# Attention b's stream: each query group divided by its sums in four small parts, a batch's output given out in three passes

## The chip, the core and the metric

The kernel runs on one core of a Trainium2 chip. The core has a matrix engine (TensorE, called PE in the profile, with its weight loads as PEld), three engines for elementwise work (VectorE or DVE, ScalarE or ACT, GpSimd or POOL) and DMA queues, of which this kernel uses the one of SyncE (SP). Matmul results go to PSUM[...]. The metric is the device time of one execution in microseconds, lower is better.

## What is computed

Two layers on x of 2 batches x 512 tokens x 512 values, all fp32, each layer an attention and then a small mixture of experts, each with a layer norm ahead and added to x:

```python
x = x + attn_a(layernorm(x))    # 32 heads of 128, 8 key heads, 4-bit weights, rope, causal
x = x + ffn(layernorm(x))       # 8 experts of rank 64, the best two of a softmax gate
x = x + attn_b(layernorm(x))    # 32 heads of 16, 8 key heads, rope, causal
x = x + ffn(layernorm(x))
```

The change lies in attention b and in what is laid beside it:

```python
att = einsum('bhgqd,bhkd->bhgqk', q, k) / sqrt(16)      # g: the 4 query heads of a key head
probs = softmax(where(causal, att, -inf))
out = einsum('bhgqk,bhkd->bhgqd', probs, v)
return concat_heads(out) @ Wo
```

## The kernel before

Attention a comes first (to about 720 us), then the first experts ("f1"), then attention b, then the second experts ("f2").

**Units of attention b.** A unit is (batch b, query group g of 4, half kh of the key heads): 2 x 4 x 2 = 16 units, 4 heads in each, one on each strip of 32 partitions. Two streams walk the units. `maxima` (lines 653 to 676) multiplies queries by keys (`sc_b`, L668) and takes the row maxima on DVE (L672) into a spare column of `qpads`. `probabilities` (681 to 712), some 8 steps later, makes the transposed scores less the maximum (`st_b`, L694), takes exp on ACT (L700) and clears the part over the diagonal on POOL (L704). Both take their PSUM banks from the one pool `ps_x` of five banks, so a score that has not been read yet keeps the next from being made. `weighted_b` (714 to 745) multiplies the probabilities by the values (`num_b`, L721). The values carry a column of ones, so the row sums come out as row 16 of each strip.

**Sums and division.** When a unit's four products are done, ACT copies the result to SBUF: for kh = 0 into `oN[b, g]`, for kh = 1 into a temporary tile. Four DMAs on SP's queue bring the four rows of sums into a tile `dens` (L738), and for kh = 1 four more bring the values beside those of kh = 0 (L745). Before the change one tile `dens[b, 0]` collects the sums of the groups 0 to 2 of a batch and `dens[b, 1]` those of group 3, each after a memset on POOL (L735). `divided(b, late)` (747 to 757) takes the reciprocal of such a whole 128x512 tile on DVE (L750), then for each of its groups spreads the rows over the strips (`stream_shuffle`, L755) and multiplies (L756).

**Output.** `output_b(b)` (759 to 769) first runs `divided(b, 1)`, then for each of 4 token tiles accumulates the four groups' products with `wo2` in one PSUM bank `po` (L764) and adds it to x on DVE (L768).

**The order.** The loop of lines 798 to 835 goes through 104 steps (96 of 16 units x 6, and LEAD = 8 more), with `half` = 48. Inside it the order on PE is the written order (`manual_schedule`); the order on the other engines is made by the planner that builds the program. A step does two pieces of each stream, two thirds of a `weighted_b` (the queue `due`), and side work: a generator `side`, whose parts name their cost (0.9 for some 0.86 us of matmuls), is advanced until the `pace` of the step is used up:

```python
            left += pace
            while left > 0:
                got = next(side, None)
                if got is None:
                    left = 0.0
                else:
                    left -= got
```

Side work is first the rest of batch 1's first experts and its projections (pace 1.35, to step 46), then nothing until step 59, then batch 0's output and second experts (pace 1.25). `divided(0, 0)` is run whole at step 49, `divided(1, 0)` at step 97. After the loop come batch 1's output, what is left of the side work, and batch 1's second experts (840 to 844). Outside the loop the planner orders PE too. A part of the projections puts rotations on DVE (L579, L581); an experts' layer begins with a norm, whose square root makes ACT load another table.

Of the kernel before, what the change touches and what calls it, by code (L numbers as in the profile page):

```python
# [11 lines left out]
F32 = mybir.dt.float32  # L12
# [3 lines left out]
ALU = mybir.AluOpType  # L16
# [3 lines left out]
P = 128  # L20
B, S, DM = 2, 512, 512
# [10 lines left out]
B_NH, B_NKV, B_HD = 32, 8, 16  # L32
B_G = B_NH // B_NKV
# [8 lines left out]
def kernel(  # L42
# [21 lines left out]
    nc = tc.nc  # L64
# [63 lines left out]
    with ExitStack() as actx:  # L128
# [192 lines left out]
        def chain(*stages):  # L321
            for stage in stages:
                yield from stage
# [11 lines left out]
        for n in range(len(units) + 4):  # L335
            turn = []

            def at(lag):
                if 0 <= n - lag < len(units):
                    g, b, h = units[n - lag]  # L340
                    return (g, b, h, f"{g}_{b}_{h}")

            if at(3):
                g, b, h, nm = at(3)
# [4 lines left out]
            if at(0):  # L349
                g, b, h, nm = at(0)  # L350
# [8 lines left out]
            if at(4):  # L359
                g, b, h, nm = at(4)  # L360
                turn.append(output(wo[g], h, g * A_G + h, b, *ats.pop((g, b, h)), nm))
            if at(2):
                g, b, h, nm = at(2)
# [37 lines left out]
    wo2 = w2.tile([P, B_G, DM], F32, tag="wo2", name="wo2")  # L401
# [32 lines left out]
    temps = ctx.enter_context(tc.tile_pool(name="temps", bufs=4))  # L434
    wep = ctx.enter_context(tc.tile_pool(name="we", bufs=2))
    gate = ctx.enter_context(tc.tile_pool(name="gate", bufs=1))
    bp = ctx.enter_context(tc.tile_pool(name="b", bufs=1))
# [9 lines left out]
    def bank(shape, name):  # L447
        pool, tag = (ps_x, "x") if shared["on"] else (ps_f, "f")
        return pool.tile(shape, F32, tag=tag, name=name)
# [4 lines left out]
    MM = 0.9  # L454
# [136 lines left out]
    def projections(b):  # L591

        xT = yield from norm_parts(b, "b")


        kT = kTs[b] = bp.tile([P, 2, S], F32, tag=f"kT{b}", name=f"kT_b_{b}")
        v = vpads[b]
        for t in range(NT):
            nm = f"b_{b}_{t}"
            kpad = kpads[t % 2]  # L600
            pq = bank([P, DM], f"pq_{nm}")
            for c in range(NC):
                nc.tensor.matmul(  # L603
                    pq, xT[:, c, ts(t, P)], wq2[:, c, :], start=(c == 0), stop=(c == NC - 1)
                )
                if c == NC - 1:
                    rope_heads(qpads[b, t], pq, B_NH, t, 2, f"q{nm}")
                yield MM
            pkv = bank([P, DM], f"pkv_{nm}")
            for c in range(NC):  # L610
                nc.tensor.matmul(
                    pkv[:, :256], xT[:, c, ts(t, P)], wkv2[:, c, :], start=(c == 0), stop=(c == NC - 1)
                )
                if c == 1:
                    yield MM
            rope_heads(kpad, pkv[:, 0:128], B_NKV, t, 0, f"k{nm}")
            for kh in range(2):
                nc.scalar.copy(
                    v[:, t, kh, :, :B_HD],
                    pkv[:, 128 + kh * 64 : 192 + kh * 64].rearrange("p (s d) -> p s d", d=B_HD),  # L620
                )
            yield 3 * MM
            tp = bank([P, 2, P], f"tpk_{nm}")
            kf = kpad.rearrange("p h d -> p (h d)")
            for c in range(2):
                nc.tensor.transpose(tp[:, c, :], kf[:, ts(c, P)], ident)
            nc.scalar.copy(kT[:, :, ts(t, P)], tp)
            yield 0.2
# [18 lines left out]
    STEPS, LEAD, HELD = 6, 8, 1  # L647
    qTm, qTp, nums, oNs = {}, {}, {}, {}


    dens = {}
# [62 lines left out]
    def weighted_b(b, g, j, kh, pT):  # L714


        first, last = j == 0, j == NT - 1
        if first:
            nums[b, g, kh] = ps_n.tile([P, S], F32, tag="num", name=f"num_b_{b}_{g}_{kh}")
        for s in range(4):  # L720
            nc.tensor.matmul(  # L721
                nums[b, g, kh][ts(s, STRIP), j * P :], vpads[b][:, j, kh, s, :], pT[s],
                start=first, stop=last,
            )
        if not last:
            return
        if kh == 0:
            got = oNs[b, g] = bp.tile([P, S], F32, tag=f"oN{b}{g}", name=f"oN_b_{b}_{g}")
        else:
            got = temps.tile([P, S], F32, tag="t", name=f"o1_b_{b}_{g}")  # L730
        nc.scalar.copy(got, nums.pop((b, g, kh)))
        row, late = kh * B_G + g, int(g == B_G - 1)
        if (b, late) not in dens:
            dens[b, late] = bp.tile([P, S], F32, tag=f"dens{late}", name=f"dens_b_{b}_{late}")
            nc.gpsimd.memset(dens[b, late], 1.0)  # L735
        for s in range(4):
            at = s * STRIP
            nc.sync.dma_start(  # L738
                dens[b, late][at + row : at + row + 1, :], got[at + B_HD : at + B_HD + 1, :]
            )  # L740
        if kh == 1:

            for s in range(4):
                at = s * STRIP
                nc.sync.dma_start(oNs[b, g][at + B_HD : at + STRIP, :], got[at : at + B_HD, :])  # L745

    def divided(b, late):

        rden = temps.tile([P, S], F32, tag="t", name=f"rden_b_{b}_{late}")
        nc.vector.reciprocal(rden, dens[b, late])  # L750
        yield 5.0
        for g in (B_G - 1,) if late else range(B_G - 1):
            rb = temps.tile([P, S], F32, tag="t", name=f"rb_b_{b}_{g}")
            rows = [kh * B_G + g for kh in range(2) for _ in range(B_HD)]
            nc.vector.stream_shuffle(rb, rden, rows)  # L755
            nc.vector.tensor_tensor(oNs[b, g], oNs[b, g], rb, ALU.mult)  # L756
            yield MM

    def output_b(b):
        yield from divided(b, 1)  # L760
        for i in range(NT):
            po = bank([P, DM], f"po_{b}_{i}")
            for g in range(B_G):
                nc.tensor.matmul(  # L764
                    po, oNs[b, g][:, ts(i, P)], wo2[:, g, :], start=(g == 0), stop=(g == B_G - 1)
                )
                if g == B_G - 1:
                    nc.vector.tensor_tensor(x[b, i], x[b, i], po, ALU.add)  # L768
                yield MM

    def run(*stages):
        stages = list(stages)
        while stages:
            stages = [st for st in stages if next(st, stages) is not stages]
# [5 lines left out]
    def parts(stage, n):  # L780
        for _ in range(n):
            next(stage, None)
# [10 lines left out]
    total = len(units) * STEPS  # L793
    half = total // 2
    shared["on"] = False
    side = chain(later, projections(1))
    pace, left, col = 1.35, 0.0, 0.0
    for step in range(total + LEAD):
        with tc.manual_schedule(engines={mybir.EngineType.PE}):
            if step == half - 2:  # L800
                run(side)
            for b in range(B):

                if step == half * (b + 1) + 1:
                    run(divided(b, 0))
            if step == half + LEAD + 3:
                side = chain(output_b(0), experts(0, "f2", True))
                pace, left = 1.25, 0.0
            for lead in (0, 2):
                k, at = divmod(step + lead, STEPS)  # L810
                if at == 0 and k < len(units) and (lead or step == 0):
                    qTm[units[k]] = transposed(*units[k], "m")
            k, at = divmod(step - STEPS, STEPS)
            if at == 1 and 0 <= k < len(units):
                qTp[units[k]] = transposed(*units[k], "p")

            alone = step < LEAD or step >= total
            for _ in range(4 * (step % 2 == 0) if alone else 2):
                if LEAD <= step:
                    next(ps)  # L820
                if step < total:
                    next(ms)

            col += 2 / 3
            while col >= 1:
                col -= 1
                if len(due) > HELD:
                    due.pop(0)()
# [7 lines that stand above are left out]
    shared["on"] = True  # L836
    while due:
        due.pop(0)()

    last = output_b(1)  # L840
    parts(last, 2)
    parts(side, 5)
    run(last)
    run(side, experts(1, "f2", True))


# [88 lines left out]
```

## Time and profile before

| | us |
|---|---|
| median of 3 runs | 1170.47 (1168.96 to 1172.08) |
| the profiled execution | 1172.71 |
| its span | 1170.7 |
| PE busy | 1107.2 |
| DVE busy | 883.0 |
| ACT busy | 591.7 |
| POOL busy | 525.5 |
| mean granted clock of PE | 0.975 of full speed |

A profile is one execution. "Busy" is the time in which an engine had an instruction running. PE's matmuls overlap and their ends are modelled, so a busy PE may still run below its best. The granted clock is the share of full speed that the chip gave PE; at 0.50 each matmul takes twice as long. A line of the timeline gives the start in us from the span's start, the duration, the engine, the source line and operation, what it writes and reads, the shape, and in brackets how long the engine had stood before it and what ended that. One fp32 matmul of the source is two records. Of attention b's stream, 812 us to 1110 us are the loop; the two streams overlap from 830 to 1085.

### The profile page before, as it was taken

The page shows a single profiled execution, that of the slowest core. Times are in us where ns is not written, and L with a number is a line of the kernel's source. Part 1 is how long each engine was busy: PE and PEld are TensorE (multiplying, and loading weights), DVE is VectorE, ACT ScalarE, POOL GpSimd, SP SyncE. Part 2 cuts the span into 40 slices and gives each one's busy share as a digit, 9 for nine tenths or more (in the row PEclk, how much of TensorE's full clock was granted, in tenths as well). Part 3 has the DMA queues.
Part 4 walks back from the last instruction along what each step waited for, and adds up shares of the span by engine and source line. Part 5 has one row for each costly group of instructions (what it writes and reads, how often), then busy time and mean ns, then how long its engine had stood idle before and what let it go on. Part 6 is the DMA issues. An engine that isn't in the chain of part 4 may idle for free.

```text
span 1170.7 us, 16843 instructions
## 1 busy us (share of the span) xinstructions
PE 1107.2 (95%) x5428; PEld 694.0 (59%) x5428; DVE 883.0 (75%) x2175; ACT 591.7 (51%) x1373; POOL 525.5 (45%) x758
## 2 busy tenths in 40 slices
PE   5799999999999999999999996989999999999998
PEld 3467777777777776777777774444444444444343
DVE  6889899998998999999998887244755676565442
ACT  3566566576656656656566663212254444364410
POOL 1556655665565666566565665111123322222200
PEclk9999999999999999999999998899989978989999
DMA  7301011022001100101100002400000000000000
GB/s 274 108 1 37 1 37 37 1 72 72 3 35 37 37 1 37 38 1 37 37 1 1 1 1 92 76 0 1 2 1 6 6 6 6 7 6 2 15 32 36
DMA packets 13448, 35.07 MB, mean 30 GB/s; under 512 B 4081, under 2 KB 5041, under 8 KB 10801
## 3 DMA queue, kind: packets, MB, share of 16 engines
q1 hardware_dynamic: 13360, 34.01, 8.8%
q8 instruction: 43, 0.70, 0.2%
q14 instruction: 45, 0.36, 0.1%
HBM read 30.72 MB, written 2.10 MB: 28 GB/s over the span
## 4 chain that ended last, share of the span: by engine, by line
PE 86%; DVE 7%; ACT 2%; POOL 2%; issue 2%; DMA 1%; SPq 0%; DVEq 0%; ACTq 0%; POOLq 0%
PE av L280 11%; PE sc L247 11%; PE st_b L694 7%; PE tp L275 6%; PE ps_o L289 5%; PE ps_o L290 5%; PE ps_q L209 5%; PE py_f L563 5%; PE ps_q L210 5%; PE ph_f L504 4%; PE num_b L721 4%; PE po L764 3%; PE pq_b L603 3%; PE sc_b L668 2%; PE ps_k L210 1%
## 5 line engine op out<-in xcount | busy, mean ns | idle before, releaser
L672 DVE CUSTOM_DVE_ANT_0 sc_b<-sc_b,tri 128x128 f32<-128x128 f32 (+3 forms) x256 | 122.6, 510 | 92.2 <-PE sc_b L668 76.6
L255 ACT ACTIVATE p<-sc,nmx 128x128 f32<-128x128 f32 (+3 forms) x256 | 135.5, 529 | 93.9 <-DVE nmx L250 91.8
L247 PE MATMUL sc<-kT,qT 128*128 128x128 f32 (+3 forms) x512 | 179.6, 433 | 1.5 <-POOL qT L228 1.2
L216 DVE SCALAR_TENSOR_TENSOR r_q<-ps_q,s_q,r_q 128x512 f32<-128x512 f32 x192 | 143.7, 749 | 35.8 <-PE ps_q L210 22.4
L227 POOL TENSOR_TENSOR r_q<-r_q,tab 128x512 f32<-128x512 f32 x64 | 82.3, 1286 | 191.1 <-DVE rs_q L226 191.1
L276 ACT COPY pT<-tp 128x128 f32<-128x128 f32 (+3 forms) x256 | 109.3, 427 | 102.2 <-PE tp L275 101.5
L264 POOL TENSOR_SCALAR p<-p,rden 128x128 f32<-128x128 f32 (+3 forms) x256 | 139.2, 556 | 46.2 <-DVE rden L262 22.8
L704 POOL TENSOR_SCALAR_AFFINE_SELECT pT_b<-pT_b 128x128 f32<-128x128 f32 (+1 forms) x192 | 62.7, 331 | 195.2 <-ACT pT_b L700 192.5
L280 PE MATMUL av<-pT,v 128*128 128x512 f32 (+3 forms) x512 | 148.7, 433 | 0.2 <-ACT pT L276 0.2
L280 PEld LDWEIGHTS av<-pT,v 128*128 128x128 f32 x512 | 96.8, 190 | 80.6 <-issue 52.7
L700 ACT ACTIVATE pT_b<-st_b 128x384 f32<-128x384 f32 (+1 forms) x192 | 92.2, 528 | 96.3 <-PE sc_b L668 68.1
L299 DVE SCALAR_TENSOR_TENSOR acc<-ps_o,s_o,acc 128x512 f32<-128x512 f32 x186 | 137.7, 740 | 2.9 <-PE ps_o L290 2.7
L209 PE MATMUL ps_q<-xh,w_q 128*128 128x512 f32 x256 | 122.8, 480 | 7.4 <-DVE r_q L216 7.4
L250 DVE CUSTOM_DVE_ANT_0 sc<-sc,tri 128x128 f32<-128x128 f32 (+3 forms) x256 | 125.7, 491 | 3.5 <-PE sc L247 2.5
L694 PE MATMUL st_b<-qT_b_p,kT_b 32*128 32x256 f32 (+3 forms) x512 | 119.1, 503 | 6.0 <-DVE qpad L672 3.6
L668 PE MATMUL sc_b<-kT_b,qT_b_m 32*128 32x384 f32 (+3 forms) x512 | 118.2, 499 | 1.4 <-ACT qT_b_m L639 0.7
L275 PE MATMUL tp<-ident,p 128*128 128x128 f32 x640 | 112.7, 272 | 2.3 <-POOL p L264 2.3
L247 PEld LDWEIGHTS sc<-kT,qT 128*128 128x128 f32 x512 | 95.3, 189 | 24.3 <-POOL qT L228 1.6
L289 PE MATMUL ps_o<-ah,w_o 128*128 128x512 f32 x256 | 108.3, 424 | 1.1 <-ACT ah L168 0.9
L290 PE MATMUL ps_o<-al,w_o 128*128 128x512 f32 x256 | 103.4, 407 | 3.5 <-DVE al L169 3.5
L210 PE MATMUL ps_q<-xl,w_q 128*128 128x512 f32 x256 | 101.5, 396 | 0.0
L275 PEld LDWEIGHTS tp<-ident,p 128*128 128x128 f32 x640 | 82.8, 140 | 28.9 <-issue 4.8
(175 smaller groups left out, 2010.6 us busy)
## 6 DMA issues: line engine op xcount, KB each, us to landing
codes_q<-in_q_codes_dram SPq DMA_DIRECT2D x8, 1024.0 KB, 4.8
codes_o<-in_o_codes_dram SPq DMA_DIRECT2D x8, 1024.0 KB, 4.8
x_a<-in_x_dram SPq DMA_DIRECT2D x8, 256.0 KB, 6.6
codes_k<-in_k_codes_dram SPq DMA_DIRECT2D x2, 1024.0 KB, 6.3
codes_v<-in_v_codes_dram SPq DMA_DIRECT2D x2, 1024.0 KB, 6.0
x_r<-in_x_dram SPq DMA_DIRECT2D x8, 256.0 KB, 3.5
out_dram<-x_r SPq DMA_DIRECT2D x8, 256.0 KB, 2.1
la<-in_lora_a_dram SPq DMA_DIRECT2D x1, 1024.0 KB, 5.6
```

The lines of the kernel that those rows point to most:

```text
L209: nc.tensor.matmul(ps, w[:, c, ts(h, A_HD)], xh[b][:, c, :], start=True, stop=False)
L210: nc.tensor.matmul(ps, w[:, c, ts(h, A_HD)], xl[b][:, c, :], start=False, stop=True)
L216: nc.vector.scalar_tensor_tensor(r, ps, s, r, ALU.mult, ALU.add)
L247: nc.tensor.matmul(sc[:, :n], qT[:, ts(i, P)], kT[:, :n], start=True, stop=True)
L264: nc.gpsimd.tensor_scalar(prs[j], prs[j], rden[:, j % 2 : j % 2 + 1], 1.0, ALU.mult, ALU.mult)
L275: nc.tensor.transpose(tp[:, j, :], prs[i][:, ts(j, P)], ident)
L280: nc.tensor.matmul(av[:, j * P :], v[:, j, :], pT[:, j, j * P :], start=(j == 0), stop=(j == NT - 1))
L289: nc.tensor.matmul(ps, w[:, h, ts(n, P)], ah, start=True, stop=False)
L290: nc.tensor.matmul(ps, w[:, h, ts(n, P)], al, start=False, stop=True)
L299: nc.vector.scalar_tensor_tensor(to, ps, s, to, ALU.mult, ALU.add)
L668: nc.tensor.matmul(part, qT[strip, ts(i, P)], kT[strip, kh, :n], start=True, stop=True)
L694: nc.tensor.matmul(st[:, at : at + n], kT[strip, kh, ts(j, P)], qT[strip, j * P :], start=True, stop=True,)
```

## The change

The tile `dens` becomes one for each query group and batch (two tags in turn). As soon as a group's second half is done, a generator `divided(b, g)` for it is put into a list `quotients`; each step of the loop advances every generator in the list by one part: two empty parts, the reciprocal of the left 256 columns, that of the right 256, the shuffle, the product. Nothing is divided whole inside the loop any more.

`output_b(b, gs)` makes the output of the groups `gs` only and adds it to x. Batch 0's output comes in three passes: groups 0 and 1 from step 46 (pace 0.6), group 2 chained behind at step 56, group 3 at step 66 with the second experts (pace 1.05). Batch 1's groups 0 and 1 are set ahead of the side work at step 96 (pace 1.6), groups 2 and 3 follow after the loop, behind the last quotient and six parts of side work.

```diff
-        row, late = kh * B_G + g, int(g == B_G - 1)
-        if (b, late) not in dens:
-            dens[b, late] = bp.tile([P, S], F32, tag=f"dens{late}", name=f"dens_b_{b}_{late}")
-            nc.gpsimd.memset(dens[b, late], 1.0)
+        if kh == 0:
+            dens[b, g] = bp.tile([P, S], F32, tag=f"dens{g % 2}", name=f"dens_b_{b}_{g}")
+            nc.gpsimd.memset(dens[b, g], 1.0)
         for s in range(4):
             at = s * STRIP
             nc.sync.dma_start(
-                dens[b, late][at + row : at + row + 1, :], got[at + B_HD : at + B_HD + 1, :]
+                dens[b, g][at + kh : at + kh + 1, :], got[at + B_HD : at + B_HD + 1, :]
             )
...
-    def divided(b, late):
-
-        rden = temps.tile([P, S], F32, tag="t", name=f"rden_b_{b}_{late}")
-        nc.vector.reciprocal(rden, dens[b, late])
-        yield 5.0
-        for g in (B_G - 1,) if late else range(B_G - 1):
-            rb = temps.tile([P, S], F32, tag="t", name=f"rb_b_{b}_{g}")
-            rows = [kh * B_G + g for kh in range(2) for _ in range(B_HD)]
-            nc.vector.stream_shuffle(rb, rden, rows)
-            nc.vector.tensor_tensor(oNs[b, g], oNs[b, g], rb, ALU.mult)
+            quotients.append(divided(b, g))
+
+    quotients = []
+
+    def divided(b, g):
+        for _ in range(2):
             yield MM
-
-    def output_b(b):
-        yield from divided(b, 1)
+        rden = temps.tile([P, S], F32, tag="t", name=f"rden_b_{b}_{g}")
+        for n in range(2):
+            part = ts(n, S // 2)
+            nc.vector.reciprocal(rden[:, part], dens[b, g][:, part])
+            yield MM
+        rb = temps.tile([P, S], F32, tag="t", name=f"rb_b_{b}_{g}")
+        nc.vector.stream_shuffle(rb, rden, [kh for kh in range(2) for _ in range(B_HD)])
+        yield MM
+        nc.vector.tensor_tensor(oNs[b, g], oNs[b, g], rb, ALU.mult)
+
+    def output_b(b, gs):
         for i in range(NT):
-            po = bank([P, DM], f"po_{b}_{i}")
-            for g in range(B_G):
+            po = bank([P, DM], f"po_{b}_{i}_{gs[0]}")
+            for g in gs:
...
-                if g == B_G - 1:
+                if g == gs[-1]:
                     nc.vector.tensor_tensor(x[b, i], x[b, i], po, ALU.add)
                 yield MM
...
             if step == half - 2:
                 run(side)
-            for b in range(B):
-
-                if step == half * (b + 1) + 1:
-                    run(divided(b, 0))
-            if step == half + LEAD + 3:
-                side = chain(output_b(0), experts(0, "f2", True))
-                pace, left = 1.25, 0.0
+                side = output_b(0, (0, 1))
+                pace, left = 0.6, 0.0
+            if step == half + LEAD:
+                side = chain(side, output_b(0, (2,)))
+            if step == half + LEAD + 10:
+                side = chain(side, output_b(0, (3,)), experts(0, "f2", True))
+                pace, left = 1.05, 0.0
+            if step == total:
+                side = chain(output_b(1, (0, 1)), side)
+                pace, left = 1.6, 0.0
+            quotients[:] = [q for q in quotients if next(q, None) is not None]
...
-    last = output_b(1)
-    parts(last, 2)
-    parts(side, 5)
-    run(last)
+    run(*quotients)
+    parts(side, 6)
+    run(output_b(1, (2, 3)))
     run(side, experts(1, "f2", True))
```

More of the change, by code (lines that the diff above doesn't have):

```diff
@@ L745, in weighted_b @@
                 nc.sync.dma_start(oNs[b, g][at + B_HD : at + STRIP, :], got[at : at + B_HD, :])
-    def divided(b, late):
-        rden = temps.tile([P, S], F32, tag="t", name=f"rden_b_{b}_{late}")
-        nc.vector.reciprocal(rden, dens[b, late])
-        yield 5.0
-        for g in (B_G - 1,) if late else range(B_G - 1):
-            rb = temps.tile([P, S], F32, tag="t", name=f"rb_b_{b}_{g}")
-            rows = [kh * B_G + g for kh in range(2) for _ in range(B_HD)]
-            nc.vector.stream_shuffle(rb, rden, rows)
-            nc.vector.tensor_tensor(oNs[b, g], oNs[b, g], rb, ALU.mult)
-            yield MM
-    def output_b(b):
-        yield from divided(b, 1)
+            quotients.append(divided(b, g))
+    quotients = []
+    def divided(b, g):
+        for _ in range(2):
+            yield MM
+        rden = temps.tile([P, S], F32, tag="t", name=f"rden_b_{b}_{g}")
[8 more added lines that the diff above has]
+    def output_b(b, gs):
         for i in range(NT):
-            po = bank([P, DM], f"po_{b}_{i}")
-            for g in range(B_G):
+            po = bank([P, DM], f"po_{b}_{i}_{gs[0]}")
+            for g in gs:
                 nc.tensor.matmul(
-                    po, oNs[b, g][:, ts(i, P)], wo2[:, g, :], start=(g == 0), stop=(g == B_G - 1)
+                    po, oNs[b, g][:, ts(i, P)], wo2[:, g, :], start=(g == gs[0]), stop=(g == gs[-1])
                 )
-                if g == B_G - 1:
+                if g == gs[-1]:
                     nc.vector.tensor_tensor(x[b, i], x[b, i], po, ALU.add)
```

## The prediction

> **What bounds the kernel now.** I read the page first (shares of the span, then the 40 slices), then PE's waits, then the order of time around each `divided`, then busy time and clock in 2 us windows.
>
> ```profile
> PE 1107.2 (95%) x5428; PEld 694.0 (59%) x5428; DVE 883.0 (75%) x2175; ACT 591.7 (51%) x1373; POOL 525.5 (45%) x758
> PEclk9999999999999999999999998899989978989999
> ```
>
> PE is the bound, DVE is not. The dips of the granted clock lie only in attention b's stream (812 to 1110 us). Three of its five dips follow a `divided`. In order of time (us from the span's start, duration, engine, line, what, idle before it):
>
> ```profile
> 944.80 0.66 PE L638 MATMUL tpq_b_p<-ident,qpad 128*128 128x128 f32 x4
> ...
> 945.86 3.35 DVE L750 RECIPROCAL rden_b<-dens_b 128x512 f32<-128x512 f32 x1 [1.11 <-DMA dens_b<-o_b]
> ...
> 947.79 0.59 PE L668 MATMUL sc_b<-kT_b,qT_b_m 32*128 32x512 f32 x1
> ...
> 949.13 0.41 DVE L672 CUSTOM_DVE_ANT_0 sc_b<-sc_b,tri 128x256 f32<-128x256 f32 x1
> ...
> 949.65 1.22 PE L694 MATMUL st_b<-qT_b_p,kT_b 32*128 32x512 f32 x1 [1.27 <-DVE qpad L672]
> ```
>
> The reciprocal holds DVE for 3.35 us. The row maxima (L672) queue behind it, their PSUM banks don't come free, and PE, which runs on for 2.5 us (945.86 to 948.38), then stands for 1.27 us. What follows costs more (PE, PEld, DVE, ACT, POOL busy, clock, DMA share, GB/s):
>
> ```profile
> 948.00:950.00 2.00, 0.73 (x4) 0.35 (x4) 2.00 (x5) 0.60 (x1) 0.73 (x2) 0.89 0.01 2
> 950.00:952.00 2.00, 1.72 (x4) 0.15 (x2) 2.00 (x7) 0.19 (x1) 0.40 (x2) 0.50 0.00 0
> 962.00:964.00 2.00, 2.00 (x16) 1.63 (x13) 0.90 (x5) 1.22 (x3) 0.52 (x2) 0.69 0.04 9
> ...
> 982.00:984.00 2.00, 0.40 (x1) 0.41 (x2) 2.00 (x8) 0.00 (x0) 0.78 (x2) 0.93 0.01 2
> 992.00:994.00 2.00, 2.00 (x12) 0.95 (x11) 0.00 (x0) 0.58 (x1) 0.00 (x0) 0.51 0.00 0
> ...
> 1090.00:1092.00 2.00, 0.86 (x9) 0.16 (x8) 1.96 (x3) 0.58 (x1) 0.79 (x2) 1.00 0.07 16
> 1094.00:1096.00 2.00, 2.00 (x10) 0.50 (x9) 2.00 (x6) 0.00 (x0) 0.61 (x1) 0.50 0.00 0
> ```
>
> After each stop the clock is 0.50: 949.65 to 963.3, 983.6 to 994.0, 1093.4 to 1096.4. The unit from the transpose at 944.80 shows the whole price, since the next unit has the same work and no `divided`:
>
> ```profile
> 965.89 0.66 PE L638 MATMUL tpq_b_p<-ident,qpad 128*128 128x128 f32 x4
> ...
> 977.73 0.66 PE L638 MATMUL tpq_b_p<-ident,qpad 128*128 128x128 f32 x4
> ```
>
> 21.09 us against 11.84: 9.25 us lost.
>
> **What is removed.** Three divisions inside the stream, each priced as PE's stop plus half of the half-clock stretch. `divided(0, 0)`: 1.27 + 0.74 (a second stop, 951.72 to 952.46) + 13.65/2 = 8.8. `divided(0, 1)`: 2.28 + 10.4/2 = 7.5. `divided(1, 0)`, where no maxima are left: 2.05 + 3.0/2 = 3.6. Sum 19.9. The fourth (1114 us) is hidden by 32 records of `po`: nothing.
>
> Here the Trainium skill ("TensorE: Matmul & The Clock Gate", Why this matters for your kernels) speaks against me: it asks for no PE gaps over about 3 us, since one idle window costs the full clock. By that rule stops of 1.27 to 2.28 us leave the clock alone and the removal is worth 1.27 + 0.74 + 2.28 + 2.05 = 6.3 us. The rows show 0.50 after 1.27 us of standing. I take 19.9.
>
> **What is added on DVE.** A reciprocal of 128x4 took 178 ns, one of 128x512 3352: 6.25 ns an element and 0.153 fixed, so one of 128x256 takes 1.75 us. There are 4 whole ones before and 16 halves after: 28.0 - 13.4 = +14.6 us. Shuffles (0.72) and products (0.69) stay 8 each. Batch 0 is added to `x` in three passes, batch 1 in two: 20 adds in place of 8, 12 x 0.689 = +8.3. Sum +22.9 us of DVE work, which was at 5 to 7 us in each 10 there. Work as such is covered by DVE's idle time; how long one hold is decides. PE ran on 2.5 us under the whole reciprocal, so a hold of 1.75 us ends before PE would stop. The nearest row for such a hold are the rotations between maxima, with PE never idle:
>
> ```profile
> 887.14 0.69 DVE L579 TENSOR_TENSOR rc_qb<-pq_b,tabb 128x512 f32<-128x512 f32 x1
> 887.75 0.74 DVE L581 TENSOR_TENSOR rs_qb<-pq_b,tabb 128x256 f32<-128x256 f32 x2
> 888.41 0.69 DVE L672 CUSTOM_DVE_ANT_0 sc_b<-sc_b,tri 128x512 f32<-128x512 f32 x1
> ...
> 880.00:890.00 10.00, 10.00 (x66) 4.59 (x65) 6.00 (x21) 3.63 (x7) 2.82 (x7) 1.00 0.03 8
> ```
>
> That is 1.36 us of hold at no cost. But two halves come in two following steps: a step takes 17.26/6 = 2.88 us with side work (1002.62 to 1019.88 between two equal `num_b`), its two maxima take 1.3, a half 1.75, so each step is left 0.2 us behind, and side work on DVE (0.7) makes it 0.9. The second half can then stop PE for up to 0.9 us. Below, nothing; I take 0.6 for each of the six quotients that fall between maxima and 0.4 for (1, 2): +4.0, ends 0 and +7. None of these alone is as long as the 1.27 us stop above. The skill ("VectorE: DVE Perf Modes", the errata section) advises tiles of 512 elements or more; by it the halves cost 8 x 0.153 = 1.2 us of DVE time against whole reciprocals. That is true and off the path, while a whole one outlasts PE's 2.5 us.
>
> **Waits, queues, memory.** The two empty steps ahead of a reciprocal stand for the DMAs of the sums: at 942.15 four issues of 0.6 us, then 1.7 us to landing, 4.8 us from the last `num_b`; two steps and their remainder are 5 to 8 us, in the thin steps 46 to 58 about 5. Up to 1 us of DVE's 1.11 us wait can therefore remain for (0, 2), with the maxima queued behind; it is in the 4.0. DMAs are as many as before on SP's queue, and in the same place. POOL gets four memsets more (0.52 us each), behind selects that idle for ACT: nothing, at worst 2 us later sums, which the empty steps take. The single matmul passes take a bank of `ps_f` each, shared with transposes; at one part a step and an add of 0.69 us, nothing.
>
> **What moves on PE.** Matmuls are the same 64 records. Side work by `pace`: before, the side work from step 59 is a division (5.0 + 0.9), sixteen parts of `po` and the experts (7.0 + 42 parts), a part at 0.9: 65.1 units. The 45 steps 59 to 103 take 45 x 1.25 = 56.3, so nine parts (the 10 + 8 records of `py_f` seen at the end) and sixteen of `po` are left for the tail: 25. After: three queries of batch 0 in steps 46 to 65, then in steps 66 to 95 30 x 1.05 = 31.5 of 3.6 + 44.8 = 48.4, then 8 x 1.6 = 12.8 of the rest and 7.2 for batch 1's first pass, 24.1; 11.3 units or 12.5 parts are left, and eight of `po`: 20.5. The tail loses 4.5 x 0.86 = 3.9 us (0.86: 32 records of `po` took 13.73 in the chain). In the stream a part costs less than 0.86: 17.26 - 11.84 = 5.4 us for 8.3 parts, 0.65. So 4.5 x 0.65 = +2.9. Eight parts move into the steps 46 to 58, which carry none now; were the first parts of a unit nearly free there, -3 more. I take -2 in all, ends -5 and 0.
>
> At the end the last quotient takes copy 0.6, issues 2.4, landing 1.7, halves 3.5, shuffle and product 1.4: 9.6 us after `num_b`. It is covered by six side parts (5.2) and four `po` of query 2 (3.4): +1.0 us of waiting, unless the planner draws later parts ahead. The sqrt loads of ACT (stops at 857 and 1028, clock 0.50 after each) stay.
>
> Sum: -19.9 + 4.0 - 2 + 1 = -16.9 us. Against the profiled execution (1172.71, span 1170.7) 1155.8; it lay 2.2 above the median of the runs, 1170.47, so 1153.6.
>
> **Rivals.**
> Likeliest (0.58): as summed, 1153.6, own range 1148 to 1160.
> More (0.14): holds cost nothing and the thin steps hide most of what is moved in: -19.9 - 5 = about 1145.5. For it: the rotations at full clock. Against: DVE's load in steps 25 to 40, where rotations and quotients meet.
> Half (0.18): two quotients still stop PE long enough for the clock, (0, 2) with its DMA wait and one among the rotations, 7.5 each: -16.9 + 15 - 1.2 = -3, but with dense side work the clock recovers sooner (3.0 us at 1093), so 1163. For it: at 1028.3 a stop of 0.70 us after ACT's loads was enough.
> Slower (0.10): the change doesn't part the reciprocals. Only PE's order is held as written; DVE's is the planner's, and both halves are ready at once. If they run back to back, a quotient is again a hold of 3.5 us, and there are six amid maxima in place of two: six at the mean of 8.8 and 7.5, 8.2, and 3.6 for (1, 2), less 19.9 and 1: +32 us if all do. It decides from three held whole (3 x 8.2 > 20.9); with four, about 1184. Against: a part is written per step, and after 949.13 DVE mixed maxima between shuffles.
>
> **How the numbers follow.** A measurement of this kernel can tell about 0.3% (3.5 us) from no change. Likeliest, More and two thirds of Half lie below 1167: faster 0.84. The rest of Half: same 0.06. Slower 0.10. The range 1142 to 1168 leaves out the slower case and small ends of the others.
>
> **What would show it.** Right: no DVE instruction of this part over 1.8 us, no clock of 0.50 near quotients, a unit without rotations near 17 us throughout, less than 22 records of `py_f` between the stream's end and batch 1's norm plus 16 of `po`. Wrong: halves adjacent on DVE; PE waiting on `qpad` over 1.2 us; a clock of 0.50 after (0, 2); PE standing before the last `po`.

## The result, and the profile after

The changed kernel takes 1164.72 us, median of 9 runs (1160.68 to 1167.5), beside 1171.71 for the kernel before on the same chip (9 runs): ratio 0.9937, 95% interval 0.9915 to 0.9959. Timed a second time, on another chip, it took 1161.17 beside 1171.34: 0.9913 (0.9891 to 0.9935). So it is faster, as forecast, by 7 to 10 us where I forecast 16.9. The profiled execution took 1160.68 us with a span of 1159.0 and a mean granted clock of 0.982; it was the fastest of the nine, so differences below that are read from profiles flatter the change by some microseconds against its median.

The page's shares of the span and its row of the granted clock:

```profile
PE 1096.3 (95%) x5428; PEld 686.5 (59%) x5428; DVE 899.4 (78%) x2199; ACT 591.4 (51%) x1373; POOL 530.1 (46%) x762
PEclk8999999999999999999999999799989999899999
```

PE is still the bound. Its busy time fell by 10.9 us with the same records, as fewer of them ran at half clock (mean granted clock 0.982, before 0.975). DVE's busy time rose by 16.4 us. Summed by instruction, its reciprocals and its adds to `x` rose by 22.4 us (27.7 - 13.4 and 13.6 - 5.5), beside the 22.9 of the prediction; a part of the difference is that neighbours on DVE overlap (two halves in a row take 3.37 us, not 3.50). In attention b's stream the 7 and the 8 in the slices from 937 and 966 us, at the first two divisions, have become 9s. An 8 from 840 us and one from 985 us remain; they are not the divisions': the clock is at 0.50 from 859 to 866 and from 1006 to 1014, after ACT's table loads for the square roots (two of 1.28 us, from 854.60 and from 1001.68), as it was after those loads before. One stretch of 0.50 is new, from 1020 to 1023, inside a slice that the row shows as 9.

At the place of the old first stop the order of time is now this (start, duration, engine, line, what, idle before it and what ended that):

```profile
945.80 1.75 DVE L758 RECIPROCAL rden_b<-dens_b 128x256 f32<-128x256 f32 x1 [1.11 <-DMA dens_b<-o_b]
...
948.49 0.92 PE L668 MATMUL sc_b<-kT_b,qT_b_m 32*128 32x128 f32 x4 [1.18 <-DVE qpad L672]
...
948.68 1.74 DVE L758 RECIPROCAL rden_b<-dens_b 128x256 f32<-128x256 f32 x1
...
976.95 1.75 DVE L758 RECIPROCAL rden_b<-dens_b 128x256 f32<-128x256 f32 x1 [1.89 <-DMA dens_b<-o_b]
...
979.63 0.92 PE L668 MATMUL sc_b<-kT_b,qT_b_m 32*128 32x128 f32 x4 [1.96 <-DVE qpad L672]
```

The half takes the 1.75 us that I worked out. But PE stops again, for 1.18 us at the same quotient (0, 2) and 1.96 us at (0, 3), waiting for the same row maxima. The windows (PE, PEld, DVE, ACT, POOL busy, clock, DMA share, GB/s) show what does not come back:

```profile
946.00:948.00 2.00, 1.31 (x16) 0.94 (x14) 2.00 (x6) 1.27 (x3) 0.38 (x2) 1.00 0.23 53
948.00:950.00 2.00, 1.51 (x12) 0.67 (x12) 2.00 (x6) 0.19 (x1) 0.28 (x1) 1.00 0.00 0
950.00:952.00 2.00, 2.00 (x13) 0.85 (x10) 2.00 (x10) 0.00 (x0) 0.88 (x2) 1.00 0.00 0
...
978.00:980.00 2.00, 0.36 (x3) 0.37 (x4) 2.00 (x10) 0.55 (x2) 0.41 (x1) 1.00 0.16 37
980.00:982.00 2.00, 2.00 (x14) 0.60 (x12) 2.00 (x5) 0.00 (x0) 0.37 (x1) 1.00 0.00 0
```

The clock stays at 1.00 after both stops, where it was 0.50 after the stop of before.

### The profile page after: what moved, and what is told of

Same layout as the page of the kernel before. It is cut to its first block, busy times and chain, and to the rows that moved or that the text cites. A ratio compares the mean times of both kernels' runs of the same rounds, so it can differ in the third digit from the quotient of the medians.

```text
span 1159.0 us, 16881 instructions
## 1 busy us (share of the span) xinstructions
PE 1096.3 (95%) x5428; PEld 686.5 (59%) x5428; DVE 899.4 (78%) x2199; ACT 591.4 (51%) x1373; POOL 530.1 (46%) x762
## 4 chain that ended last, share of the span: by engine, by line
PE 84%; DVE 9%; ACT 2%; issue 2%; POOL 2%; DMA 1%; SPq 1%; DVEq 0%; ACTq 0%; POOLq 0%
PE av L280 11%; PE sc L247 11%; PE st_b L694 6%; PE tp L275 5%; PE ps_o L289 5%; PE ps_o L290 5%; PE ps_q L209 5%; PE py_f L563 5%; PE ps_q L210 5%; PE ph_f L504 4%; PE num_b L721 3%; PE pq_b L603 3%; PE sc_b L668 2%; PE po L770 2%; DVE r_q L216 1%
## 5 line engine op out<-in xcount | busy, mean ns | idle before, releaser
L216 DVE SCALAR_TENSOR_TENSOR r_q<-ps_q,s_q,r_q 128x512 f32<-128x512 f32 x192 | 143.4, 747 | 35.8 <-PE ps_q L210 22.4
L668 PE MATMUL sc_b<-kT_b,qT_b_m 32*128 32x384 f32 (+3 forms) x512 | 113.6, 481 | 4.8 <-DVE qpad L672 3.4
L694 PE MATMUL st_b<-qT_b_p,kT_b 32*128 32x256 f32 (+3 forms) x512 | 107.0, 478 | 2.5 <-ACT pT_b L700 1.7
```

Source lines behind the costliest of these rows:

```text
L216: nc.vector.scalar_tensor_tensor(r, ps, s, r, ALU.mult, ALU.add)
L668: nc.tensor.matmul(part, qT[strip, ts(i, P)], kT[strip, kh, :n], start=True, stop=True)
L694: nc.tensor.matmul(st[:, at : at + n], kT[strip, kh, ts(j, P)], qT[strip, j * P :], start=True, stop=True,)
```

## The experiments

Two questions stood open: which term of the sum lost 7 to 10 us, and why. The theory that I began with was that the halves still stop PE, because DVE's order is the planner's and puts them ahead of maxima that PE waits for. Against it stood that the moved output passes gain less than I took, or that the removed stops were worth less than 19.9. All ratios below are to the kernel before, timed beside it on the same chip; where the intervals of two ratios overlap I do not tell the two apart.

**The changed kernel again**, beside the next three.

> The changed kernel once more, for a second profile of it; 1171.7 us is the kernel before, 1164.7 the changed one. Theory A (the first halves of (0, 2), (0, 3) and (1, 1) stand in DVE's queue ahead of maxima that were written before them, and wait there for the DMA of the sums): the same halves wait again, 0.5 to 2 us, PE stops 1 to 2 us behind those of (0, 2) and (0, 3); if this execution is slower than 1162, a clock of 0.50 follows one of the two stops, which it did not in the first profile. Theory B (the added 22.9 us of DVE work cost, wherever they lie): stops of 0.3 to 0.9 us spread over all six quotients. Theory C (the removed stops were worth less than the 19.9 us of one profile): no stop of PE behind a quotient is worth a microsecond. Time 1161 to 1168 by all.

Measured: 1161.17 us (6 runs, 1159.85 to 1164.32); the next three were timed on the same chip. In its profiled execution (1164.32 us) PE stopped in the same two places:

```profile
950.28 0.92 PE L668 MATMUL sc_b<-kT_b,qT_b_m 32*128 32x128 f32 x4 [1.19 <-DVE qpad L672]
...
981.70 0.92 PE L668 MATMUL sc_b<-kT_b,qT_b_m 32*128 32x128 f32 x4 [2.23 <-DVE qpad L672]
```

DVE had waited 1.12 and 2.16 us for the sums there. The clock stayed at 1.00 behind both stops, so theory A's 0.50 in a slower execution did not come.

**Parting taken back.** A quotient runs whole in one step, so that its halves are neighbours on DVE; the passes stay.

```diff
-            quotients[:] = [q for q in quotients if next(q, None) is not None]
+            run(*quotients)
+            quotients.clear()
```

> The changed kernel, but all parts of a quotient are written at one point, one step after its sums are sent for; the planner then sets the two halves next to each other. Passes and paces as in the changed kernel. A: the hold is the wait plus 3.5 us, for six quotients; PE stops 2 to 3 us at each, the clock falls to 0.50 at three or more, 1172 to 1190 us. B: the same DVE work, the same time, 1162 to 1168. C: halves side by side cost a microsecond or two each, 1166 to 1172.

Measured: 1170.36 us (22 runs), 0.9994 (0.998 to 1.0008): nothing of the gain is left. Its timeline at the first quotient, then its windows there:

```profile
877.86 3.36 DVE L758 RECIPROCAL rden_b<-dens_b 128x256 f32<-128x256 f32 x2 [0.48 <-DMA dens_b<-o_b]
...
882.60 2.23 PE L475 MATMUL pxT_b<-ident,xn_b 128*128 128x128 f32 x8 [4.21 <-DVE xn_b L470]
```

```profile
880.00:882.00 2.00, 0.00 (x0) 0.00 (x0) 2.00 (x6) 0.00 (x0) 0.52 (x1) 0.60 0.01 2
882.00:884.00 2.00, 1.36 (x6) 1.00 (x7) 2.00 (x6) 0.25 (x1) 0.00 (x0) 0.50 0.00 0
```

Two halves in a row (3.36 us) stand ahead of the norm's part that PE needs: a stop of 4.21 us, with the clock at 0.50 from 882 to 886. This one unit takes 23.7 us, where it takes 17.0 in the second profile of the changed kernel: 6.7 us, as much as the two spans differ (1169.1 and 1162.6). That is the mechanism of my slower rival, mostly in one place. The edit takes back the two empty parts as well, so it does not show the parting alone. And at (0, 2) a longer hold behind the same wait gave a shorter stop than 1.18 us:

```profile
953.29 3.37 DVE L758 RECIPROCAL rden_b<-dens_b 128x256 f32<-128x256 f32 x2 [1.11 <-DMA dens_b<-o_b]
...
955.35 0.92 PE L668 MATMUL sc_b<-kT_b,qT_b_m 32*128 32x128 f32 x4 [0.55 <-ACT pT_b L700]
```

The score waited here for ACT's exp, not for a row maximum. Whom a score waits for thus depends on the order as a whole; I take it that the planner gave it another of the five banks of `ps_x`, which is not shown. The units of (0, 2) and (0, 3) still took 0.6 and 2.0 us longer than in the second profile of the changed kernel.

**Halves held behind the maxima.** Each half first copies the newest row maximum into a spare column, so that the planner cannot set it ahead of that maximum. The column is read and has no effect on the result.

```diff
...
-            part = ts(n, S // 2)
-            nc.vector.reciprocal(rden[:, part], dens[b, g][:, part])
+            part = ts(n, S // 2 + 1)
+            col = n * (S + 1)
+            nc.vector.tensor_copy(dens[b, g][:, col : col + 1], newest[0])
+            nc.vector.reciprocal(rden[:, part], dens[b, g][:, part])
```

> The changed kernel, but each half first copies the newest row maximum (128x1) into a spare column of the tile of sums and takes the reciprocal of that column too, so that the planner can't set it ahead of the maxima that were written before it. 16 copies of 128x1 more, all else the same. A: the halves of (0, 2), (0, 3) find their sums landed or wait under 0.5 us with no maximum behind them that has its scores, PE's stops of 1.2 and 2.0 us go, and with them the clock falls of slower executions: 1155 to 1162. B: the same work and 2 us of copies more: 1164 to 1168. C: as B.

Measured: 1165.31 us, 0.9942 (0.9919 to 0.9965): no gain, where theory A had 1155 to 1162. DVE's wait ahead of the first half of (0, 2) fell from 1.11 to 0.25 us, yet PE still stopped for 1.03 us at 950.83, behind the second half and the shuffle. At (0, 3) the stop fell from 1.96 to 0.73 us. But from 1050 to 1058 the clock was at 0.50, and that unit took 24.0 us where the changed kernel kept 1.00 and took 19.5. So the theory that the place alone does it fell: moved later, a half stands before other maxima.

**No early passes.** The parts stay; all four groups of batch 0 go out in one pass from step 66, and steps 46 to 65 carry no side work.

```diff
...
-                side = output_b(0, (0, 1))
-                pace, left = 0.6, 0.0
-            if step == half + LEAD:
-                side = chain(side, output_b(0, (2,)))
...
-                side = chain(side, output_b(0, (3,)), experts(0, "f2", True))
-                pace, left = 1.05, 0.0
+                side = chain(output_b(0, (0, 1, 2, 3)), experts(0, "f2", True))
+                pace, left = 1.41, 0.0
```

> The changed kernel, but batch 0's output is given out in one pass of four groups from step 66, at a pace of 1.41 to step 95 so that as much side work is done by step 96 as in the changed kernel; steps 46 to 65 carry none. Eight adds fewer on DVE. If the fill of the thin steps is worth what I took (2 to 5 us): 1167 to 1170. If parts cost 0.65 us wherever they lie: 1163 to 1166. Theory A: with nothing beside them the steps 46 to 58 go faster, so the waits for the sums of (0, 2) and (0, 3) grow to 1.5 to 2.5 us and the stops with them; B: eight adds fewer, 1 to 3 us less.

Measured: 1175.53 us (14 runs, 1168.62 to 1178.38), 1.002 (1.000 to 1.004), above all that was expected. The parting without batch 0's early passes gains nothing. In the profiled execution (1170.19 us), the timeline and windows at quotient (0, 2):

```profile
945.91 1.75 DVE L758 RECIPROCAL rden_b<-dens_b 128x256 f32<-128x256 f32 x1 [1.11 <-DMA dens_b<-o_b]
...
948.19 0.66 PE L694 MATMUL st_b<-qT_b_p,kT_b 32*128 32x512 f32 x1 [1.02 <-DVE qpad L672]
...
950.58 0.69 PE L668 MATMUL sc_b<-kT_b,qT_b_m 32*128 32x512 f32 x1 [1.26 <-DVE qpad L672]
...
953.00 1.22 PE L694 MATMUL st_b<-qT_b_p,kT_b 32*128 32x512 f32 x1 [0.81 <-DVE qpad L672]
```

```profile
950.00:952.00 2.00, 1.42 (x6) 0.59 (x6) 1.97 (x9) 0.46 (x1) 0.77 (x3) 0.97 0.00 0
952.00:954.00 2.00, 1.19 (x4) 0.51 (x4) 2.00 (x6) 0.60 (x1) 0.29 (x1) 0.50 0.00 0
954.00:956.00 2.00, 2.00 (x12) 0.20 (x8) 1.00 (x4) 0.60 (x1) 0.23 (x1) 0.50 0.00 0
```

The same half, with the same wait, and a stop as long as the 1.18 us of the changed kernel; but with no products of `po` around it PE stops three times in 6 us, and the clock falls to 0.50. So the parts gain only together with batch 0's early passes.

**No reciprocals, after and before.** Both kernels without the reciprocal of attention b's sums: the shuffle spreads a tile of ones instead (`ones`, set once on POOL). The division is left out of the computation. The edit of the changed kernel:

```diff
...
-            nc.vector.reciprocal(rden[:, part], dens[b, g][:, part])
...
-        nc.vector.stream_shuffle(rb, rden, [kh for kh in range(2) for _ in range(B_HD)])
+        nc.vector.stream_shuffle(rb, ones, [kh for kh in range(2) for _ in range(B_HD)])
```

> The changed kernel without its reciprocals: the shuffles read a tile of ones, so the division is left out; passes, paces, DMAs, shuffles and products stay. What it is under the changed kernel (1161 to 1165 us) is the whole price of the sixteen halves and of their waits. If the shortfall of some 8 us against my sum lies in the holds (theory A or B): 1153 to 1157. If it lies in what the removed stops were worth, or at the end (theory C): 1159 to 1162, the 4 us that I took for the holds and no more.

> The kernel before without its reciprocals: the shuffles read a tile of ones, so the division is left out; the rest as before (1171.4 us). It measures my term of 19.9 us for the removed stops by itself. If that was right: 1150 to 1154, less a microsecond or two for shuffles and products that still come at one point. Theory C: 1158 to 1166, since the steps without side work have slack that takes part of the half clock up.

Measured: 1152.2 us (5 runs, 1151.66 to 1152.87; 0.9836, 0.9816 to 0.9856) for the changed kernel, and 1158.91 (0.9895, 0.9875 to 0.9914) for the kernel before, which took 1171.7 beside them. These two make the ledger: all divisions of before are worth 1171.7 - 1158.91 = 12.8 us, the rest of the change (passes, pace, end, shuffles and products in parts) 1158.91 - 1152.2 = 6.7, and the 16 halves cost 9.0 (1161.17 - 1152.2) to 12.5 (1164.72 - 1152.2). The changed kernel was timed on two other chips than these, whose kernels before lay within 0.4 us of 1171.7. In the kernel before without reciprocals one long stop behind a quotient remains:

```profile
974.12 0.69 DVE L756 TENSOR_TENSOR oN_b<-oN_b,rb_b 128x512 f32<-128x512 f32 x1 [1.96 <-DMA oN_b<-o_b]
...
975.66 1.22 PE L696 MATMUL st_b<-qT_b_p,kT_b 32*128 32x512 f32 x1 [2.31 <-DVE qpad L674]
```

The product waits 1.96 us for the DMA of the values, with maxima behind it. I had put the stop of about this length in this place (2.28 us) down to the reciprocal of `divided(0, 1)`.

**One DMA for the four rows of sums** in place of four issues of 0.6 us.

```diff
-        for s in range(4):
-            at = s * STRIP
-            nc.sync.dma_start(
-                dens[b, g][at + kh : at + kh + 1, :], got[at + B_HD : at + B_HD + 1, :]
-            )
+        nc.sync.dma_start(dens[b, g][kh :: STRIP, :], got[B_HD :: STRIP, :])
```

> The changed kernel with the four rows of sums of a unit fetched by one DMA in place of four, so that the sums land about 1.8 us sooner. A: the waits of the halves of (0, 2) and (0, 3) (1.1 and 1.9 us) fall under 0.5 us and PE's stops behind them under 0.8: 1158 to 1162. B or C: no wait in the sum, so the changed kernel's 1161 to 1165 again.

Measured: 1162.41 us, 0.9919 (0.9899 to 0.9939): not to be told from the changed kernel. The planner used the earlier sums to set the halves earlier, and with a wait of DVE for the sums of 1.6 us in all in place of 5.5, PE still stopped for 1.49 us at 948.72 and at 980.02. Theory A had these stops under 0.8. With the wait gone it was the second half that did it at (0, 2):

```profile
946.53 1.75 DVE L754 RECIPROCAL rden_b<-dens_b 128x256 f32<-128x256 f32 x1
...
948.72 0.92 PE L668 MATMUL sc_b<-kT_b,qT_b_m 32*128 32x128 f32 x4 [1.49 <-DVE qpad L672]
```

The first half, at 943.60, and an add to `x` had left DVE behind with the maxima when the second began.

**Halves that wait for no DMA.** The 16 halves keep their length but read a tile of ones, so the true sums are left out.

```diff
...
-            nc.vector.reciprocal(rden[:, part], dens[b, g][:, part])
+            nc.vector.reciprocal(rden[:, part], ones[:, part])
```

> The changed kernel with halves of the same length that read a tile of ones, so that none waits for a DMA; the division is left out, the DVE work is all there, and the planner may set the halves earlier. A: most of the holds' price is the wait, 1157 to 1161. B: as the changed kernel, 1161 to 1165, with e9 far below it.

Measured: 1157.58 us (5 runs, 1155.93 to 1158.01; 0.9878, 0.986 to 0.9897). The work of the halves by itself, in the order that the planner gave it here, costs 1157.58 - 1152.2 = 5.4 us (the same chip); that they wait for sums, and stand where the sums come, costs the other 3.6 to 7.1. The halves of (0, 2) were neighbours here (3.36 us from 940.01), and PE stopped only 0.79 us behind them: the same 3.36 us that cost 4.21 us of standing in another place.

```profile
940.01 3.36 DVE L760 RECIPROCAL rden_b<-ones 128x256 f32<-128x256 f32 x2
...
943.94 0.92 PE L670 MATMUL sc_b<-kT_b,qT_b_m 32*128 32x128 f32 x4 [0.79 <-DVE qpad L674]
```

**Sums spread over the partitions.** If what counts is the length of what stands before a maximum, the reciprocal should be made short. Of the 128x512 tile only 8 rows carry sums: 4096 values, which are 128x32. Here DMA brings them in that form, one reciprocal does them all, and two DMAs bring them back to the rows that the shuffle reads. All is computed.

```diff
-            dens[b, g] = bp.tile([P, S], F32, tag=f"dens{g % 2}", name=f"dens_b_{b}_{g}")
-            nc.gpsimd.memset(dens[b, g], 1.0)
-        for s in range(4):
-            at = s * STRIP
-            nc.sync.dma_start(
-                dens[b, g][at + kh : at + kh + 1, :], got[at + B_HD : at + B_HD + 1, :]
-            )
+            dens[b, g] = bp.tile([P, STRIP], F32, tag=f"dens{g % 2}", name=f"dens_b_{b}_{g}")
+        nc.sync.dma_start(
+            dens[b, g][kh * 64 : kh * 64 + 64, :], got[B_HD::STRIP, :]
+        )
...
-        for n in range(2):
-            part = ts(n, S // 2)
-            nc.vector.reciprocal(rden[:, part], dens[b, g][:, part])
-            yield MM
+        few = bp.tile([P, STRIP], F32, tag="few", name=f"few_b_{b}_{g}")
+        nc.vector.reciprocal(few, dens[b, g])
+        nc.gpsimd.memset(rden, 1.0)
+        for kh in range(2):
+            nc.sync.dma_start(rden[kh::STRIP, :], few[kh * 64 : kh * 64 + 64, :])
+        for _ in range(3):
+            yield MM
```

> The eight rows of sums of a query group are spread by DMA over 128 partitions x 32 columns, so that one reciprocal of 128x32 takes some 0.153 + 32 x 0.00625 = 0.35 us in place of two of 1.75; two DMAs bring the results back to the rows that the shuffle reads, and POOL sets one more 128x512 tile. All is computed. If it is the length of what stands before the queued maxima (wait and half together 2.9 to 3.6 us, over the 2.5 us that PE runs on), a wait of up to 1.9 us with 0.35 us behind it stays under that and the time is near the kernel without reciprocals: 1152 to 1155, with no stop of PE over 0.5 us near 948 and 980 us. If the waits for DMAs matter by themselves, the second wait (for the results to come back, ahead of the shuffle) brings what the halves took: 1158 to 1162, with DVE standing at a shuffle and PE stopping behind it. At the end the last quotient is about as late as before: 3.2 us less of reciprocals, some 2.5 to 3 more for the way back.

Measured: 1153.84 us (6 runs, 1150.23 to 1158.06) beside 1172.37, 0.9855 (0.9827 to 0.9883): faster than both kernels, as expected, and not to be told from the kernel that does not divide at all. One DMA for four rows of sums, which is in it too, had brought nothing by itself. Its timeline at (0, 2) and (0, 3), then its windows at (0, 3):

```profile
944.77 0.01 DVE L761 LOAD_MASK_SELECT rb_b<-rden_b  x1 [0.98 <-DMA rden_b<-few_b]
...
969.98 0.35 DVE L754 RECIPROCAL few_b<-dens_b 128x32 f32<-128x32 f32 x1 [1.00 <-DMA dens_b<-o_b]
...
973.52 0.01 DVE L761 LOAD_MASK_SELECT rb_b<-rden_b  x1 [0.56 <-DMA rden_b<-few_b]
```

```profile
970.00:972.00 2.00, 2.00 (x23) 0.86 (x19) 1.97 (x7) 1.01 (x3) 0.79 (x2) 1.00 0.22 49
972.00:974.00 2.00, 2.00 (x25) 1.23 (x24) 1.39 (x8) 1.42 (x3) 0.66 (x2) 1.00 0.05 8
974.00:976.00 2.00, 2.00 (x9) 0.78 (x10) 1.97 (x9) 0.00 (x0) 0.16 (x1) 1.00 0.00 0
```

DVE still waits for DMAs, about 1 us before the reciprocal and again before the shuffle, 10.8 us over the kernel (4.0 for the sums, 6.8 for the way back), and at these two quotients PE does not stand; in the rest of the stream no wait of PE for a maximum is over 0.57 us. By the medians, from two chips, waits of this size alone cost the 1.6 us between 1153.84 and 1152.2, which these runs cannot tell from nothing; the work of the halves alone cost 5.4; waits and halves together, ahead of the maxima, cost 9.0 to 12.5.

## Why the prediction was right and wrong

**What failed: the holds, 4.0 us, of "What is added on DVE".** They cost 9.0 to 12.5. The step said that "a hold of 1.75 us ends before PE would stop", since "PE ran on 2.5 us under the whole reciprocal". Two things in it were wrong, and one was missing.

The 2.5 us were counted from the start of the reciprocal. That cover is no constant. Counted in the same way in the changed kernel, PE runs on to 948.49 - 1.18 = 947.31, which is 1.51 us after the half began at 945.80, and to 977.67, 0.72 us after 976.95. Counted from the moment DVE stood still (945.80 - 1.11 = 944.69 and 976.95 - 1.89 = 975.06) it is 2.62 and 2.61 us, twice the same; in the kernel before the same count gives 948.38 - 944.75 = 3.63. What PE has in hand is used up from when DVE takes no more maxima, for whatever reason.

The wait for the sums I had seen, and put "in the 4.0" as up to 1 us. It adds to the hold before any maximum can run: 1.11 + 1.75 = 2.86 us and 1.89 + 1.75 = 3.64 us. Missing was that PE starts again only some maxima later, 0.94 and 0.93 us after the half's end. With that the stops are 2.86 + 0.94 - 2.62 = 1.18 and 3.64 + 0.93 - 2.61 = 1.96. These two sums are made of what they explain. The second profile tests them: with its waits they give 1.12 + 1.75 + 0.94 - 2.62 = 1.19 and 2.16 + 1.75 + 0.93 - 2.61 = 2.23, which are the stops that it shows. For a half with no wait ahead the same sum gives 1.75 + 0.93 - 2.61, about nothing, which was my case; for the spread sums 1.00 + 0.35 + 0.93 - 2.61 is below nothing, and PE does not stop. The sum holds for these two places in this kernel's order. For the halves in a row at (0, 2) it gives 1.11 + 3.37 + 0.94 - 2.62 = 2.80 us, and PE stopped for 0.55, since it waited for ACT there; the 4.21 us and 0.79 us behind 3.36 us say the same: each order needs its own count. Where the second half stops PE, as with one DMA for the sums, the step was right in kind, with 1.49 us where it had up to 0.9.

By unit, the changed kernel against the one without reciprocals, from the transposes of the queries (two views, first after, then without):

```profile
945.78 0.66 PE L638 MATMUL tpq_b_p<-ident,qpad 128*128 128x128 f32 x4
...
962.20 0.66 PE L638 MATMUL tpq_b_p<-ident,qpad 128*128 128x128 f32 x4
```

```profile
944.89 0.66 PE L640 MATMUL tpq_b_p<-ident,qpad 128*128 128x128 f32 x4
...
959.67 0.66 PE L640 MATMUL tpq_b_p<-ident,qpad 128*128 128x128 f32 x4
```

The unit of (0, 2) takes 16.42 us against 14.78: 1.6 us, a little more than the stop itself. That of (0, 3) takes 18.33 (from 976.14) against 16.25 (from 973.61), +2.1. A unit of batch 1 with quotient (1, 0) beside the norm of the second experts loses 2.3; there PE stopped for 0.81 us until 1018.40, and at 1020 to 1022 the clock was 0.50 (0.49 us and 1.00 in the same unit without reciprocals). The two units at (0, 0) lose 1.4, the one at (1, 1) 1.1, that of (0, 1) nothing, and the end 0.9. With small pieces elsewhere that is the difference of the two spans, 1159.0 - 1150.2 = 8.8 us. I had 0.6 for each of six and 0.4 for one more.

**Planner and pacing.** I argued that one part a step would keep the halves apart. Only partly: for (0, 2) four maxima lie between the halves, for (0, 1) and (1, 0) one, and for (1, 2) none, as this line of the changed kernel shows (x2 is two halves in a row):

```profile
1078.81 3.37 DVE L758 RECIPROCAL rden_b<-dens_b 128x256 f32<-128x256 f32 x2 [0.74 <-DMA dens_b<-o_b]
```

The slower rival named this cause and needed it in three places amid maxima. With all of them together the change was worth nothing (ratio 0.9994), not +32 us: the price of 8.2 us a piece, taken from before, did not hold among the passes, and most of what this run lost lay at (0, 0), beside a norm. Of the signs of being wrong that I had listed two came, halves that are neighbours and a wait on `qpad` of over 1.2 us; two did not: no 0.50 followed (0, 2), and PE did not stand before the last `po`.

**What was removed: 19.9 us, measured 12.8.** `divided(0, 0)` was nearly right: the two units from 931.7 to 965.89 took 34.2 us before, and without reciprocals the same stretch (931.0 to 957.55) 26.6: 7.6 us against my 8.8. For `divided(0, 1)`, from 965.89 to 1001.2, 35.3 us became 32.4 (957.55 to 989.91): 3.0 us against 7.5, because the product's wait for its DMA stood there as well, and stopped PE with its own half clock once the reciprocal was gone. I had looked only at the instruction that held. For `divided(1, 0)`, priced at 3.6, the time from the last unit's transposes to the end shows 2.3: 81.2 us before, 78.9 without reciprocals.

**What moved on PE: -2 and +1, measured -6.7.** The two kernels without reciprocals separate this from the divisions. From the last unit's transposes to the end of the span they take 1157.2 - 1078.3 = 78.9 us and 1150.2 - 1073.07 = 77.1: the end got shorter by 1.8, where I took 3.9 less 1.0. (With the divisions it went from 81.2 to 78.1, but there 2.3 us are `divided(1, 0)`.) The rest, some 5 us, lies ahead of it, where I took +2.9 for parts moved in and -3 for thin steps, and it is a sum of larger pieces. The units that carry the moved parts were not nearly free: 12.68 us became 14.78 and 12.03 became 13.94. The unit of the stop of 2.31 us fell from 20.33 to 16.25, and one of batch 1, from 1007 us, from 18.25 to 14.47; why that one did is not shown. The run with one pass shows one thing that I had no term for: with products of `po` laid among the thin steps, stops of 1.18 and 1.96 us passed at full clock, and without them the clock fell among stops of 1.02, 1.26 and 0.81. The stop of 2.31 us in the kernel before without reciprocals, with 0.50 from 976 to 980 behind it, stands in those thin steps too, and is gone in the changed kernel without reciprocals, where PE stops for 0.53 us there. Whether the passes took it away or the later place of the product, these two runs do not separate.

So the forecast without divisions, -19.9 - 2 + 1 = -20.9, came out at -19.5 (1152.2 against 1171.7), but by luck: two errors of some 6 to 7 us cancel; the one that did not cancel was the holds. The rival Half was near in time (1163) and named (0, 2) with its DMA wait, but at the wrong price: it gave 7.5 us to each of two quotients through the clock, and what happened is one to two microseconds at five quotients, mostly without it.

**The rule weighed.** The Trainium skill ("TensorE: Matmul & The Clock Gate", Why this matters for your kernels) let short gaps pass; I set it aside because of the 1.27 us stop of before. The runs stand between: stops of 1.18 and 1.96 us left the clock at 1.00; one of 1.26 us, between two others in the run with one pass, and one of 0.81 us did not. By the rule's 6.3 us for the removal the forecast would have been about 1167; by mine 1153.6; the divisions were worth 12.8.

What stays open: why 0.81 us were enough for the clock at 1018 and 1.96 us were not at 979 (the work of PE in the microseconds around is a likely cause, argued from the run with one pass, not isolated), which bank of the pool a score is given and so whom it waits for, and why holding the halves behind maxima lost in a later unit what it saved.

## What to carry to other kernels

A queue in order is blocked by the wait plus the instruction behind it. Compare that sum, and the first instructions that the other engine needs after it, with what that engine has in hand, counted from the moment the queue stops and not from the start of the instruction; and count it anew in each order, since the other engine may wait for something else there. Before cutting a long instruction in parts, look whether it works mostly on nothing: here 8 of 128 rows carried sums, and spreading them over all partitions made 0.35 us of 3.5 and got back what the parts had left. And when a stop is removed, look for what is late next in the same place, a DMA above all.

## What was not expected of the hardware

- The clock's answer to a stop of PE was not a matter of its length alone: 1.00 after 1.18 us (948.49) and 1.96 us (979.63), 0.50 soon after one of 0.81 us (1018.40) in the same execution. The second profile of the kernel has it again: 1.00 after 1.19 and 2.23 us, 0.50 from 1022 after 1.03 us (1020.70).
- A reciprocal of fp32 is priced by its columns: 0.35 us for 128x32, 1.75 for 128x256, 3.35 for 128x512, the same 6.25 ns a column and 0.15 us fixed throughout. The 8 of 128 partitions that carry sums do not show in it: halves that read only ones took the same 1.74 us on average.
- A row of 512 sums spread over 16 partitions by DMA (8 KB for four rows, in one issue of 0.59 us on the way back) came back soon enough that the detour through DMA cost no time that these runs can tell: 1153.84 against 1152.2 with no division.
